# A two-layer graph network on one NeuronCore: stage 1 written out as one order on three engines, and the MLP's input transposed by DMA

## The chip, the core and the metric

The kernel runs on one core of a Trainium2 chip. The core has a matrix engine (TensorE, PE in the profile; its weight loads are PEld), three other compute engines (VectorE or DVE, ScalarE or ACT, GpSimd or POOL) and an engine that only issues DMAs here (SyncE or SP). Each engine takes its own instructions in order; engines wait for one another by semaphores. The metric is the time of one execution on the device, in microseconds (us). Three runs of the kernel before took 2258.7, 2261.97 and 2261.64 us; their median is 2261.64 us.

## The reference, cut to what matters

There are N = 3327 nodes with 1024 features. Two layers follow one another.

```python
# layer 0: a quantised graph convolution
h = relu(layernorm(x))
h_q = round(min(h / act_alpha, 1) * 15) / 15 * act_alpha
w_q = sign(wc) * round(abs(wc) * 7) / 7 * wgt_alpha   # wc = clip((w - mean(w)) / std(w) / wgt_alpha, -1, 1)
support = relu(h_q @ w_q)                             # 3327x1024 @ 1024x1024
x = x + adj @ quantise(support)                       # adj: 3327x3327
# layer 1: eight-head graph attention and an MLP
h = relu(layernorm(x))
Wh = einsum('nf,hfd->hnd', h, W)                      # 8 heads of 64
e = leaky_relu(e_src[:, :, None] + e_dst[:, None, :], 0.2)
att = softmax(where(adj > 0, e, NEG))
enc = elu(att @ Wh) laid side by side                 # 3327x512
x = x + mlp(enc)                                      # 512 -> 256 -> 256 -> 512 -> 1024, relu between
```

## The kernel before

Nodes are cut into T = 26 tiles of 128 rows. The program has four stages, one after another on PE:

1. **Stage 1, support (to about 135 us).** The weight w (1024 x 1024) is loaded as eight slices of 128 rows; its mean and variance are taken by DVE (L341) and, for slices 2 and 5, by ACT (L259 to L263). After that each slice, one 512-column half at a time, is rounded to small integers (wb, int8; ACT at L415 or DVE at L413) and clamped (w_int, bf16; DVE or GpSimd, L417 and L419). Node tiles come in pairs (GT = 2): `load` reads two tiles of x, `measure` takes their statistics on DVE, `normalise` turns these into a scale and a bias in a chain over GpSimd, ACT (root, L131) and DVE (reciprocals). `to_bytes` (ACT, L286) rounds a tile to bytes (xb), `quantise` clamps it on DVE (xq, L296) and transposes it (xqt): tile 0 by eight PE transposes (L304) and an ACT copy (L305), tiles 1 to 25 by a DMA transpose on SP. Then there are sixteen products for each tile on PE (`product`, L430: two halves of eight slices), an eviction by ACT (sb, L456) and a clamp by DVE into s_int.
2. **Stage 2 (to about 942 us)**: adj @ s_int (L568), the residual, layer norm, the transposition of each tile as two planes of 16-bit halves (`transposed_by_dma`: ACT copy yh at L475, DMA transpose, ACT copy ht at L479) and the heads' products (L502).
3. **Stage 3, attention (to about 1954 us)**: head by head, over columns in two subsets of seven and six tiles; masked rows are built by DVE (sel, L867) and multiplied by PE (acc, L876). Each of 32 closes ends in the activation of its rows and a DMA by GpSimd into enc_d, a DRAM buffer of 32-bit words [nodes, 512]. In the last steps the MLP's first group of four tiles is started in between (`first_layer`: transposes at L822, copies at L827, products at L832).
4. **Stage 4, MLP (to about 2252 us)**: seven groups, six of four tiles and one of two. For each, SP loads enc_d and the residual rows (`load_nodes`), PE transposes enc (L935, 16 for a full group) and ACT copies it to enct (L938), then `dense` three times (products at L910, eviction h by ACT at L917), and the last layer (o, L947) with the residual added by DVE (L957) and stored by SP.

What sets the order: `pin` (`tc.keep_in_program_order`) keeps an instruction in the order in which it is written on its engine. Before, the weight's instructions on ACT and DVE are pinned, the first tiles' steps stand between them by a table (`between`), and the products and later tiles are placed by the scheduler, which decides each engine's order when it builds the program. x0's normalisation (L131, L132, L138, L165, L166) is not pinned. The first three tiles' products are written half by half (half 0 of tiles 0, 1, 2, then half 1). The pool of xq tiles has 2 buffers, that of xqt 4, PSUM has 3 tiles for products and 1 for transposes.

Of the kernel before, what the change touches and what calls it, by code (L numbers as in the profile page):

```python
# [8 lines left out]
F32 = mybir.dt.float32  # L9
# [11 lines left out]
P = 128  # L21
# [4 lines left out]
F = 1024  # L26
# [34 lines left out]
def two_layer_kernel(  # L61
# [42 lines left out]
    enc_d = dram.tile([NP, EMB], F32, name="enc_d")  # L104

    const.tile([P, 152], F32, name="gap")
# [4 lines left out]
    def reciprocal(t, name):  # L111
        r = const.tile([P, 1], F32, name=name)
        nc.vector.reciprocal(r, t)
        return r

    def scaled(t, c, name):
        r = const.tile([P, 1], F32, name=name)
        nc.vector.tensor_scalar(r, t, c, None, ALU.mult)
        return r

    def load_rows(dst, ap, t):

        if rows_of(t) < P:
            nc.vector.memset(dst, 0.0)
        for r in row_pieces(t):
            nc.sync.dma_start(dst[r], ap[t * P + r.start : t * P + r.stop, :])

    def half_inverse(v, n, tag, engine=nc.vector):

        s, r, q = (small.tile([P, n], F32, tag=tag + c, name=tag + c) for c in "srq")  # L130
        nc.scalar.activation(s, v, AF.Sqrt)  # L131
        nc.vector.reciprocal(r, s)  # L132
        if n == 1:
            nc.vector.scalar_tensor_tensor(q, v, r, s, ALU.mult, ALU.add)
        else:
            engine.tensor_tensor(q, v, r, ALU.mult)
            engine.tensor_tensor(q, q, s, ALU.add)
        nc.vector.reciprocal(r, q)  # L138
        return r

    def statistics(stats, src):
        for c in range(FC):
            nc.vector.bn_stats(stats[:, c, :], src[:, c * 512 : (c + 1) * 512])

    def plus_eps(var, n, tag, engine=nc.vector):
        v = small.tile([P, n], F32, tag=tag + "v", name=tag + "v")
        engine.tensor_scalar(v, var, EPS, None, ALU.add)
        return v

    def normalised(dst, src):  # L150

        stats = small.tile([P, FC, 6], F32, tag="stats", name="stats")
        statistics(stats, src)
# [3 lines left out]
        r = half_inverse(plus_eps(mv[:, 1:2], 1, "ln"), 1, "ln")  # L157
        nc.vector.tensor_scalar(r, r, 2.0, None, ALU.mult)
        return ins, r

    def scale_and_bias(rs, mean, n, factor, tag, engine=nc.vector):

        nb = small.tile([P, n], F32, tag=f"{tag}n", name=f"{tag}n")
        if engine is nc.vector:
            nc.vector.tensor_scalar(rs, rs, factor, None, ALU.mult)  # L165
            nc.vector.scalar_tensor_tensor(nb, mean, -1.0, rs, ALU.mult, ALU.mult)  # L166
        else:
            engine.tensor_scalar(rs, rs, factor, -1.0, ALU.mult, ALU.mult)
            engine.tensor_tensor(nb, mean, rs, ALU.mult)
            engine.tensor_scalar(rs, rs, -1.0, None, ALU.mult)  # L170
        return rs, nb
# [11 lines left out]
    with tc.tile_pool(name="at", bufs=2, reuse_waits="tile") as atp:  # L183
# [35 lines left out]
        with tc.tile_pool(name="s1", bufs=2, reuse_waits="tile") as s1, tc.tile_pool(  # L219
            name="s1_mm", bufs=3, space=PSUM, reuse_waits="tile"  # L220
        ) as mm_ps, tc.tile_pool(name="s1_tp", bufs=1, space=PSUM, reuse_waits="tile") as tp_ps:
# [16 lines left out]
            def pair(t0):  # L238
                xs = s1.tile([P, GT, F], F32, name="xs", bufs=3)
                return xs, {t0 + q: xs[:, q] for q in range(GT)}  # L240

            def measure(mv, src, ordered=False, amid=lambda: None):

                stats = s1.tile([P, FC, 6], F32, name="stats1")
                for c in range(FC):
                    ins = nc.vector.bn_stats(stats[:, c, :], src[:, c * 512 : (c + 1) * 512])
                    if ordered:
                        pin(ins)
                    if c == 0:
                        amid()  # L250
                ins = nc.vector.bn_aggr(mv, stats.rearrange("p c s -> p (c s)"))
                if ordered:
                    pin(ins)

            def measure_on_scalar(mean, squares, src, name):

                junk = s1.tile([P, F], BF16, tag="xq", name="junk")
# [4 lines left out]
                junk = s1.tile([P, F], BF16, tag="xq", name="junk")  # L262
                pin(nc.scalar.activation(junk, src, AF.Square, bias=nmean, accum_out=squares))  # L263

            def normalise(xs, mv, t0, n, engine=nc.vector):

                v = plus_eps(mv[:, :n, 1], n, f"l0{n}", engine)
                r = half_inverse(v, n, f"l0{n}", engine)
                rs, nb = scale_and_bias(r, mv[:, :n, 0], n, to_q, f"l0{n}", engine)
                for q in range(n):  # L270
                    ready[t0 + q] = xs[t0 + q], rs[:, q : q + 1], nb[:, q : q + 1]

            def load(t0, ordered=False):
                _, xs = pair(t0)
                for t in xs:
                    load_rows(xs[t], x, t)
                mv = s1.tile([P, GT, 2], F32, name="mv")
                for q in range(GT):
                    measure(mv[:, q], xs[t0 + q], ordered)
                normalise(xs, mv, t0, GT, nc.gpsimd)  # L280


            def to_bytes(t, ordered=False):
                xs, rs, nb = ready.pop(t)
                xb = s1.tile([P, F], U8, name="xb")
                ins = nc.scalar.activation(xb, xs, AF.Relu, bias=nb, scale=rs)  # L286
                if ordered:
                    pin(ins)
                return xb

            def quantise(t, xb=None, ordered=False):
                if xb is None:
                    xb = to_bytes(t, ordered)

                xq = s1.tile([P, F], BF16, name="xq")
                ins = nc.vector.tensor_scalar(xq, xb, QA, None, ALU.min)  # L296
                if ordered:
                    pin(ins)

                xqt = s1.tile([P, KF, P], BF16, name="xqt", bufs=4)  # L300
                if t == 0:
                    tp = tp_ps.tile([P, KF, P], BF16, name="tp")
                    for k in range(KF):
                        nc.tensor.transpose(tp[:, k, :], xq[:, k * P : (k + 1) * P], ident_b)  # L304
                    pin(nc.scalar.copy(xqt, tp))  # L305
                else:
                    nc.sync.dma_start_transpose(xqt, xq)
                return xqt


            xs01, xs23, xs45 = (pair(t)[1] for t in (0, 2, 4))
            load_rows(xs01[0], x, 0)
            for k in range(KF):
                nc.sync.dma_start(w[:, k, :], w0[k * P : (k + 1) * P, :])
            for t, xs in ((1, xs01), (2, xs23), (3, xs23), (4, xs45), (5, xs45)):
                load_rows(xs[t], x, t)

            mv0, mv1, mv23, mv45 = (
                s1.tile([P, n, 2], F32, name=f"mv_{i}", bufs=1) for i, n in enumerate((1, 1, 2, 2))
            )  # L320
            measure(mv0[:, 0], xs01[0], ordered=True)
# [8 lines left out]
            normalise(xs01, mv0, 0, 1)  # L330
# [13 lines left out]
            xqts = {0: quantise(0, ordered=True)}  # L344
# [23 lines left out]
            nc.tensor.matmul(ps[:, 0:1], ones, w_mv[:, 0:1], start=True, stop=True)  # L368
# [16 lines left out]

            xbs = {}

            def rounded(t):  # L390
                xbs[t] = to_bytes(t, ordered=True)
# [611 lines left out]
```

## Time and profile before

The profiled execution took 2258.69 us; its span from the first to the last instruction is 2256.9 us, at a mean granted PE clock of 0.997.

| stage | from, us | to, us | main lines |
|---|---|---|---|
| start, until the first product | 0 | 29.1 | L341, L259, L415 |
| 1, support | 29.1 | 135.2 | L430 |
| 2, adj @ support and heads | 135.2 | 942 | L568, L502 |
| 3, attention | 942 | 1954 | L674, L867, L876 |
| 4, MLP | 1954 | 2252 | L910, L935, L947 |

| engine | busy us (share of the span) |
|---|---|
| PE | 2199.3 (97%) |
| DVE | 1532.4 (68%) |
| ACT | 1062.0 (47%) |
| POOL | 145.0 (6%) |

A row of the groups reads: line, engine, operation, output from inputs, shape, count, then busy time and the mean ns of one, then the engine's idle time just before these instructions with what ended most of it. A row of a timeline reads: start, time until the last of the run ends, engine, line, operation, count, and in brackets the engine's wait before it and what ended it. Starts of successive matmuls overlap with the ends of earlier ones, so the pace is taken from start to start.

### The profile page before, as it was taken

How to read it: one execution, taken by the hardware profiler on the slowest of the kernel's cores; microseconds unless marked ns; L12 is line 12 of the kernel's file. 1: busy time of each engine (PE TensorE's matmuls, PEld its weight loads, DVE VectorE, ACT ScalarE, POOL GpSimd, SP SyncE). 2: the span in 40 equal slices, each digit the busy share in tenths (PEclk: the TensorE clock that was granted, in tenths of full speed). 3: DMA queues.
4: the chain of work that ended last, by engine and by line, in shares of the span. 5: the costliest groups of instructions: out<-in, count | busy, mean ns of one | idle time of the engine just before them, and what ended most of it. 6: DMA issues, size and time to landing. Idle time of an engine off the chain costs nothing. (4 is left out here: it accounts for less than half of the span.)

```text
span 2256.9 us, 31286 instructions
## 1 busy us (share of the span) xinstructions
PE 2199.3 (97%) x12496; PEld 1753.9 (78%) x12496; DVE 1532.4 (68%) x1989; ACT 1062.0 (47%) x1642; POOL 145.0 (6%) x241
## 2 busy tenths in 40 slices
PE   4999999999999999899999999999999999999998
PEld 1466777777777677699999999999999999644444
DVE  7744555555555545588999999999999999722211
ACT  4634445544454454356555556555555555311120
POOL 1300111110111101000000000000000000000000
PEclk9999999999999999999999999999999999999999
DMA  6854656555665556934242331644242422443311
GB/s 208 206 188 132 188 176 182 159 163 170 181 182 168 157 162 188 311 125 146 85 135 89 108 120 46 221 162 147 81 147 85 140 84 76 143 139 117 121 56 56
DMA packets 228578, 324.56 MB, mean 144 GB/s; under 512 B 88452, under 2 KB 169300, under 8 KB 228432
## 3 DMA queue, kind: packets, MB, share of 16 engines
q1 hardware_dynamic: 208648, 249.39, 36.2%
q0 software_dynamic: 19776, 73.17, 9.9%
q8 instruction: 98, 1.61, 0.3%
q14 instruction: 48, 0.39, 0.1%
q10 hardware_dynamic: 8, 0.00, 0.0%
HBM read 216.07 MB, written 86.79 MB: 134 GB/s over the span
## 5 line engine op out<-in xcount | busy, mean ns | idle before, releaser
L867 DVE SCALAR_TENSOR_TENSOR sel<-srow,ndst,mask 128x896 fp32r<-128x896 f32 (+1 forms) x832 | 864.2, 1079 | 52.7 <-PE acc L876 47.2
L674 PE MATMUL mps<-dw,mf 128*128 128x260 f32 x2704 | 452.2, 283 | 0.1
L568 PE MATMUL mm<-s_int,hi 128*128 128x512 f32 x1352 | 427.1, 397 | 0.0
L568 PE MATMUL mm<-s_int,lo 128*128 128x512 f32 x1352 | 419.2, 391 | 0.0
L876 PE MATMUL acc<-f_even,sel 128*128 128x260 f32 x2704 | 400.2, 286 | 6.7 <-issue 5.0
L876 PE MATMUL acc<-f_odd,sel 128*128 128x260 f32 x2704 | 394.6, 286 | 0.0
L673 ACT CAST mf<-mask 128x1664 fp32r<-128x1664 uint8 x208 | 331.4, 1593 | 118.7 <-PE mps L674 100.7
L674 PEld LDWEIGHTS mps<-dw,mf 128*128 128x128 f32 x2704 | 377.0, 188 | 0.3 <-ACT part L678 0.3
L876 PEld LDWEIGHTS acc<-f_even,sel 128*128 128x128 f32 x2704 | 357.3, 190 | 11.7 <-issue 5.9
L876 PEld LDWEIGHTS acc<-f_odd,sel 128*128 128x128 f32 x2704 | 352.7, 188 | 7.3 <-issue 3.1
L568 PEld LDWEIGHTS mm<-s_int,hi 128*128 128x128 f32 x1352 | 253.9, 188 | 63.7 <-issue 12.0
L568 PEld LDWEIGHTS mm<-s_int,lo 128*128 128x128 f32 x1352 | 251.9, 188 | 51.3
L199 DVE TENSOR_SCALAR mk<-at 128x896 uint8<-128x896 f32 (+1 forms) x104 | 61.8, 596 | 225.3 <-DMA at<-in_adj_t 224.0
L502 PE MATMUL whm<-whead,ht 128*128 128x512 f32 x416 | 184.4, 596 | 6.9 <-ACT ht L479 6.8
L947 PE MATMUL o<-weights,h 128*128 128x512 f32 x416 | 179.7, 592 | 0.0
L947 PEld LDWEIGHTS o<-weights,h 128*128 128x128 f32 x416 | 79.0, 190 | 99.1 <-issue 99.0
L502 PEld LDWEIGHTS whm<-whead,ht 128*128 128x128 f32 x416 | 77.6, 190 | 100.9 <-issue 87.1
L194 ACT CAST hi<-at 128x896 fp32r<-128x896 f32 x104 | 92.5, 890 | 124.1 <-PE mm L568 87.6
L678 ACT COPY part<-mps 128x260 f32<-128x260 f32 x104 | 39.4, 378 | 223.1 <-PE mps L674 223.1
L198 DVE TENSOR_TENSOR lo<-at,hi 128x896 fp32r<-128x896 f32 x104 | 106.1, 1020 | 39.5 <-ACT hi L194 39.3
L957 DVE TENSOR_TENSOR yo<-o,nodes 128x1024 f32<-128x1024 f32 (+1 forms) x27 | 31.8, 1182 | 137.6 <-PE o L947 137.4
L430 PE MATMUL mm<-w_int,xqt 128*128 128x512 bf16 x416 | 96.5, 389 | 13.4 <-ACT sb L456 4.8
(157 smaller groups left out, 1559.2 us busy)
## 6 DMA issues: line engine op xcount, KB each, us to landing
feat_d<-fw POOLq DMA_DIRECT2D x26, 1040.0 KB, 5.3
f_even<-feat_d SPq DMA_DIRECT2D x7, 3380.0 KB, 12.3
f_odd<-feat_d SPq DMA_DIRECT2D x7, 3380.0 KB, 12.9
at<-in_adj_t SPq DMA_DIRECT2D x52, 448.0 KB, 3.5
at<-in_adj_t SPq DMA_DIRECT2D x52, 384.0 KB, 3.3
mask<-mask_d SPq DMA_DIRECT2D x39, 416.0 KB, 7.7
dw<-dsum_d SPq DMA_DIRECT2D x16, 910.0 KB, 8.8
dsum_d<-dw POOLq DMA_DIRECT2D x26, 520.0 KB, 6.2
```

The lines of the kernel that those rows point to most:

```text
L194: ins = nc.scalar.copy(hi, at)
L198: nc.vector.tensor_tensor(lo, at, hi.bitcast(F32), ALU.subtract)
L199: ins = nc.vector.tensor_scalar(mk[:, r], at, 0.0, None, ALU.is_gt)
L430: nc.tensor.matmul(mm[:, r], xqts[t][:, k, :], w_int[:, k, r], start=(k == 0), stop=(k == KF - 1))
L502: ins = nc.tensor.matmul(whm, ht[:, k, :], whead[:, k, :], start=(k == 0), stop=(k == KF - 1))
L568: nc.tensor.matmul(mm[:, c * 512 : (c + 1) * 512], which[:, q, :], s_int[j][:, c * 512 : (c + 1) * 512], start=(j == 0 and which is hi), s ...
L673: nc.scalar.copy(mf, mask[:, j : j + TH, :])
L674: nc.tensor.matmul(ps, mf[:, j % TH, :], dw[:, j, :], start=(j == 0), stop=(j == T - 1))
L678: nc.scalar.copy(part[:, i % 7], ps.rearrange("p (q c) -> p q c", q=2))
L867: nc.vector.scalar_tensor_tensor(sel[:, :nb], srow[:, :nb], ndst[:, j, h : h + 1], mask[:, :, j, :], ALU.is_gt, ALU.mult,)
L876: nc.tensor.matmul(accs[b], sel[:, b, :], f[:, j, :], start=(j == 0), stop=(j == T - 1))
L947: nc.tensor.matmul(ps[:, c * 512 : (c + 1) * 512], h3[:, k, q * P : (q + 1) * P], w4[:, k, c * 512 : (c + 1) * 512], start=(k == 0), stop= ...
```

## The change

**Stage 1.** Everything on PE, ACT and DVE is pinned, and the text is one sequence. x0's chain is pinned and stands before the weight statistics. The weight halves are written step by step (`round_weight`, `clamp_weight`): ACT rounds slices 0, 1, 3, 4, 6 and 7 of each half (before: 0, 1, 3, 4, 6), DVE slices 2 and 5 (before: 2, 5, 7); GpSimd clamps 1, 3, 5, 6, 7 of half 0 and 1, 3, 5, 6 of half 1, DVE the others. Between them stand the first tiles' steps. The scale of each pair is now a generator (`normaliser`) whose three parts are placed one by one, always with its small steps on GpSimd. Tile 0, tile 3 and all even tiles are transposed by PE and copied by ACT, 14 tiles in all; the other 12 by DMA (25 before). The first products are written as products(0,0), (1,0), (0,1), transposes of tile 2, (1,1), (2,0), transposes of tile 3, (2,1), with (tile, half); from t = 3 on a loop has one tile's products per turn, with the transposes of a later tile between its two halves. xq gets 3 buffers, the pairs' statistics 3, PSUM's transposes 2. The clearing of the last, incomplete tile moves from DVE to GpSimd.

```diff
-            def quantise(t, xb=None, ordered=False):
...
+            def by_tensor(t):
+                return t % 2 == 0 or t == 3
+
+            def quantise(t):
+
+                xq = xqs[t] = s1.tile([P, F], BF16, name="xq", bufs=3)
+                pin(nc.vector.tensor_scalar(xq, xbs.pop(t), QA, None, ALU.min))
+
+                xqts[t] = s1.tile([P, KF, P], BF16, name="xqt", bufs=4)
+                if not by_tensor(t):
+                    nc.sync.dma_start_transpose(xqts[t], xqs.pop(t))
+
+            def transpose(t):
+                tps[t] = tp_ps.tile([P, KF, P], BF16, name="tp")
+                xq = xqs.pop(t)
+                for k in range(KF):
+                    pin(nc.tensor.transpose(tps[t][:, k, :], xq[:, k * P : (k + 1) * P], ident_b))
+
+            def transposed(t):
+                pin(nc.scalar.copy(xqts[t], tps.pop(t)))
...
+            products(0, 1)
+            transpose(2)
+            products(1, 1)
+            measure(4)
+            to_bytes(3)
+            transposed(2)
+            quantise(3)
+            products(2, 0)
+            transpose(3)
+            products(2, 1)
+            load_pair(8)
+            measure(5)
+            support_bytes(0)
+            norm45 = normaliser(2)
+            transposed(3)
+            next(norm45)
+            support(0)
+            next(norm45)
+            measure(6)
+            next(norm45)
+            to_bytes(4)
+            support_bytes(1)
+            quantise(4)
+            support(1)
+            measure(7)
+            to_bytes(5)
+            load_pair(10)
+            norm67 = normaliser(3)
+            next(norm67)
+            quantise(5)
+            next(norm67)
+            measure(8)
+            next(norm67)
+            for t in range(3, T):
...
+                norm = None
+                if t % GT == 0 and t + 4 < T:
+                    norm = normaliser((t + 4) // GT)
+                    next(norm)
+                    next(norm)
+                if t + 6 < T:
+                    measure(t + 6)
+                if norm:
+                    next(norm)
+                support_bytes(t - 1)
+                support(t - 1)
+                if t + 3 < T:
+                    to_bytes(t + 3)
+                    if t % GT == 0 and t + 8 < T:
+                        load_pair(t + 8)
+                    quantise(t + 3)
+                products(t, 0)
+                ahead = 4 if t == 3 else t + 2
+                if ahead < T and by_tensor(ahead):
+                    transpose(ahead)
+                    transposed(ahead)
+                products(t, 1)
```

The first part of `normaliser` takes the sum with epsilon (GpSimd) and the root (ACT), the second the first reciprocal (DVE) and two GpSimd steps, the third the second reciprocal (DVE) and three GpSimd steps.

**Stages 3 and 4.** enc_d holds two planes of 16-bit halves. Each close makes one more ACT copy (eh) and two GpSimd DMAs instead of one. A group of the MLP is loaded transposed, by two DMA transposes on SP instead of four loads. ACT copies the planes together into enct, one group ahead; PE has no transposes there, neither in the groups nor in `first_layer`. In the program as built, the next group's four copies stand on ACT as two ahead of the second layer's first eviction, one between its two evictions and one behind them (for the last group of two tiles: three and one); the copies of groups 1 and 2, eight in all, stand ahead of group 1's first eviction.

```diff
-    enc_d = dram.tile([NP, EMB], F32, name="enc_d")
+    enc_d = dram.tile([2, NP, EMB], U16, name="enc_d")
...
+            eh = s3.tile([P, 7, HD], F32, tag="ex", name="eh").rearrange("p b d -> p (b d)")
+            eh = eh.bitcast(U16).rearrange("p (q n) -> p q n", q=2)[:, :, : nb * HD]
+            nc.scalar.copy(eh, halves_of_words(ht[:, :nb].rearrange("p b d -> p (b d)")))
+            for q in range(2):
+                nc.gpsimd.dma_start(
...
-                    for q, t in enumerate(range(t0, min(t0 + 4, T))):
-                        nc.sync.dma_start(enc[:, q, :], enc_d[t * P : (t + 1) * P, :])
+                    rows = slice(t0 * P, min(t0 + 4, T) * P)
+                    for q in range(2):
+                        nc.sync.dma_start_transpose(by_feature(enc, rows.stop - rows.start)[:, q], enc_d[q, rows])
...
+                following = s4.tile([P, EMB // P, 512], F32, name="enct")
+                n = (min(t0 + 8, T) - t0 - 4) * P
+                for k in range(EMB // P):
+                    nc.scalar.copy(
+                        halves_of_words(following[:, k, :n]),
+                        by_feature(enc_x1[(g + 1) % 2][0], n)[:, :, k],
+                    )
...
-                enct = s4.tile([P, EMB // P, 512], F32, name="enct")
-                for k in range(EMB // P):
-                    tp = ps_p.tile([P, 512], F32, tag="ps", name="tp4")
-                    for q, t in enumerate(tiles):
-                        nc.tensor.transpose(
-                            tp[:, q * P : (q + 1) * P], enc[:, q, k * P : (k + 1) * P], ident
-                        )
-                    nc.scalar.copy(enct[:, k, :cols], tp[:, :cols])
```

## The prediction

> **What bounds the kernel now.** I read the busy shares first, then the chain that ended last, then TensorE's own timeline. TensorE (PE) is busy for 97% of the span. The chain followed back from the last instruction reaches only through the MLP, and its rows there are PE's.
>
> ```profile
> PE 13%; ACT 0%; DVE 0%; DVEq 0%; issue 0%
> PE o L947 8%; PE h_ps L910 5%; PE tp L935 0%; ACT h L917 0%; ACT su L718 0%; DVE yo L957 0%; DVEq L1000 0%
> L430 PE MATMUL mm<-w_int,xqt 128*128 128x512 bf16 x416 | 96.5, 389 | 13.4 <-ACT sb L456 4.8
> ```
>
> So a microsecond is won only where PE waits or where it does work that can go. The groups name the first: 13.4 us of idle before L430, in stage 1. The change leaves the order of stages 2 and 3 alone. PE's timeline by start, length, count and wait shows stage 1:
>
> ```profile
> 29.13 0.59 PE L430 MATMUL mm<-w_int,xqt 128*128 128x512 bf16 x1 [3.54 <-DVE w_int L419]
> ...
> 33.81 6.54 PE L430 MATMUL mm<-w_int,xqt 128*128 128x512 bf16 x15 [0.57 <-POOL w_int L417]
> ...
> 58.44 24.42 PE L430 MATMUL mm<-w_int,xqt 128*128 128x512 bf16 x112 [1.21 <-DMA xqt<-xq]
> 83.02 3.61 PE L430 MATMUL mm<-w_int,xqt 128*128 128x512 bf16 x16 [0.16 <-ACT sb L456]
> 88.64 20.95 PE L430 MATMUL mm<-w_int,xqt 128*128 128x512 bf16 x96 [2.01 <-ACT sb L456]
> 110.69 24.82 PE L430 MATMUL mm<-w_int,xqt 128*128 128x512 bf16 x112 [1.09 <-ACT sb L456]
> 135.16 0.81 PE L568 MATMUL mm<-s_int,hi 128*128 128x512 f32 x2
> ```
>
> The reader is to see two paces. Fifteen products in 6.54 us are about 0.43 us each; 112 in 24.42 us are 0.216 each (a product's own 0.38 us end taken off). From 58.44 on stage 1 is PE at the second pace with 3.3 us of gaps (0.16 + 2.01 + 1.09). At 58.44, 80 products are done and 336 are left; 0.216 x 336 is 72.6, with the gaps 75.9, which ends at 134.3 against 135.16 seen. The sum closes to 0.9 us.
>
> The second removable thing is in the MLP:
>
> ```profile
> 2040.39 1.91 PE L935 MATMUL tp<-ident,nodes 128*128 128x128 f32 x16
> 2042.14 7.03 PE L910 MATMUL h_ps<-enct,weights 128*128 128x512 f32 x16
> 2049.01 10.84 PE L910 MATMUL h_ps<-h,weights 128*128 128x512 f32 x24
> ```
>
> Sixteen transposes hold PE for 1.75 us, start to start.
>
> **Stage 1, the start: -3.1 us at the scale, nothing by itself.** Before, x0's normalisation is behind weight statistics on DVE that wait for a DMA (3.41 us, to 10.59), so ACT's xb starts at 13.79. After, the chain is ahead of them: xb near 8.4, its transposed copy done near 14.7 instead of 17.9, ACT's weight statistics, which follow it in order, done near 19.9 instead of 23.0, and the weight scale at 24.0 instead of 27.1. The clamps of the two halves, redistributed over DVE and GpSimd, then end near 31.1 and 39.0, where the same walk of the old queues gives 37.4 and 47.8. This is cover: it is worth only what the node tiles can follow.
>
> **Stage 1, the ramp: this takes the gain back.** I walked the new written orders of ACT, DVE and GpSimd with the durations of before's rows (xb 1.24, sb 1.10, transposed copy 1.01, statistics half 0.67, clamp 0.69, root 0.20). At 39.1 PE has 24 products done. It does 16 more and the transposes of tiles 2 and 3 (16 x 0.216 + 16 x 0.056 = 4.4), to 43.7. Then, in order: ACT copies tile 3's transposition, to 44.9, and only behind that takes the root for tiles 4 and 5; DVE's second reciprocal comes behind tile 6's statistics, 46.6; three GpSimd steps; xb4 at 47.9, then sb1 to 50.2. DVE measures tile 7, to 52.2, before tiles 6 and 7 can have their root at 52.8; xb6 waits for their scale until 55.8; tile 4's copy stands **behind xb6** on ACT and ends at 58.0. Behind it on PE stand products(4,0) and everything later. In those 14.3 us PE has 24 products and 8 transposes, 5.6 us of work: it waits 2.8 us before tile 4's transposes and 6.0 us before products(4,0). At 58.0 only 64 products are done, so before is ahead by 16 products (3.5 us) at nearly the same moment.
>
> That such a chain is this slow is a row of before:
>
> ```profile
> 51.03 0.56 POOL L147 TENSOR_SCALAR l02v<-mv 128x2 f32<-128x2 f32 x1 [3.23 <-DVE mv L251]
> 51.62 0.20 ACT L131 ACTIVATE l02s<-l02v 128x2 f32<-128x2 f32 x1 [0.52 <-POOL l02v L147]
> 54.14 2.37 ACT L286 ACTIVATE xb<-xs,l02n,l02r 128x1024 uint8<-128x1024 f32 x2 [1.31 <-POOL l02r L170]
> ```
>
> From GpSimd's first step to xb are 3.1 us.
>
> **Stage 1, the rest.** 22 tiles are left: 22 x 16 x 0.216 = 76.0. Ten of them (6, 8, ... 24) are transposed on PE: 10 x 8 = 80 transposes. The row for eight takes 1.04 us at the slow pace (0.104 each between starts), so 0.056 at the fast one if it halves as a product does: 4.5 us. Per pair of tiles PE has 7.4 us, ACT about 5.6 and DVE about 5.4, so no gaps. 58.0 + 76.0 + 4.5 = 138.5 against 135.2: **+3.4 us**. The 13 DMA transposes fewer (25 to 12; 3.1 us each to landing) save PE nothing more: where PE waited for them, the gaps are already counted.
>
> Two rules weigh here. The Trainium skill, "TensorE: Matmul & The Clock Gate", section "Back-to-back issue gap", gives a sustained 81 ns for a pair of weight load and 128-column matmul: 80 x 0.081 is 6.5 instead of 4.5, and stage 1 would be +5.4. The row is at the slow pace, but the products' own rows halve (0.43 to 0.216); I take 0.056, with 0.104 (+3.8 more) as the upper end and 0.050 below. The same page, section "The HAM clock gate", says that the array falls to half pace after an idle window of about 3.4 us and needs about as much busy time to return. That speaks against this change: the 6.0 us wait would cost 3.4 us of work done at half pace, +1.7, or +3.4 if it falls twice. The trace has no wait over 2.01 us inside the run of products, and none of these slowed them. I take nothing, since the wait rests on my walk, and keep +3.4 for the range. Below, the ramp may be shorter (GpSimd steps of 0.2 instead of 0.3): stage 1 at 0 or, with no ramp wait at all, -5.
>
> **Attention.** Each close gets an ACT copy into two 16-bit planes and two GpSimd DMAs where there was one. The copy's nearest row is L475's, 1.90 us for 2048 columns; 32 copies of at most 896 columns are about 0.9 us each. ACT's casts in that stage wait 100.7 us for PE, which hides them; GpSimd is 6% busy. Uncovered, one copy late costs PE 0.9. The last tile's clearing moved to GpSimd, the third xq buffer and the second PSUM tile for transposes cost nothing: they only loosen waits.
>
> At the end of attention DVE finishes its last masked row at 1951.37 and PE's last products end near 1954.2, because the first layer of MLP group 0 and its transposes are mixed in (2.29 us of PE per row against DVE's 0.94). With 16 transposes gone, that layer finishes earlier, and the last eight rows have no MLP in between: PE ends about 1 us behind DVE, 1952.3: **-1.9** (0 to -1.9).
>
> **MLP.** 88 transposes on PE go: 5 x 1.75 and 0.9 for the last group of two tiles: **-9.65**. Certain.
>
> In their place ACT makes four copies per group out of DMA-transposed planes. Nearest row, the same kind of copy:
>
> ```profile
> L479 ACT COPY ht<-yht 128x2048 uint16<-128x2048 uint16 x25 | 62.6, 2506 | 85.5 <-DMA yht<-yh 85.5
> ```
>
> 1024 columns of it are about 1.28 us. They were hidden behind L938's (0.56 each) before; now they are one group ahead, but ACT issues in order, and the order puts two copies **before** the first eviction of the second layer, one between its two and one after. Before, the third layer starts its second step 4.57 us after the second layer begins (an eviction is 0.69 and waits 1 us for PE each time). After, the first layer's eviction (to +0.9), three copies and two evictions bring it to 5.89: 1.32 us of PE waiting in each of three groups, and 0.28 where the copies are of two tiles: **+4.24** (0 if they run early in ACT's long idle, +6 if a copy costs 1.45).
>
> Group 1's data is transposed from a buffer whose last write lands some 16 us after attention ends; two DMA transposes issued at 3.6 us each and landing in 5.8 are in at +25.4, eight copies done by +36, and its first layer starts at +39.4. Margin 3.4 us, cost nothing; each us past it is a us. Later groups have 47 us for two transposes. SP has them among the output stores that wait for DVE, in a queue with no other reader due within the group.
>
> **Sum.** +3.4 - 1.9 - 9.65 + 4.24 = -3.9. The profiled execution took 2258.69 us (span 2256.9); -3.9 gives 2254.8 there. Against the median of the runs, 2261.64, the same difference gives **2257.7**.
>
> **The rivals.**
> A, the forecast: the ramp and the ACT order both return part, -1.5 to -8.
> B, **the stall is not there**. The earlier scale and fewer SP transposes let node tiles follow: stage 1 at -1 instead of +3.4, or the copies cost nothing: -8.1 for either, and about -12.6 for both; near 2251. For it: before's ramp carries the same chain with PE idle 1.2 us only; against: tile 4's copy really stands behind xb6.
> C, **slower**: the clock falls in the 6.0 us wait. +3.4 in stage 1 at half pace and copies at 1.45 (+1.7): 2257.7 + 5.1 is 2262.8; with transposes at 81 ns (+2.0) and no gain in the last rows (+1.9) it is 2266.7. It decides once clock and copies add more than 3.9. For it: the rule; against: no row here.
> D, **the MLP's planes come late**: each of six groups waits for its transposes, so the change moves its 1.6 us per group from PE to a wait. 2257.7 + 5 is 2263. For it: one queue carries them with stores; against: 47 us per group.
>
> **How the numbers follow.** A 0.46 (0.26 beyond the bound, 0.20 within), B 0.33 (faster), C 0.12 (0.07 within, 0.05 slower), D 0.09 (0.08 within, 0.01 slower). A measurement of this kernel tells 0.2%, 4.5 us, from no change: below 2257.1 is faster. Faster 0.59, same 0.35, slower 0.06. The range holds A, most of B and C's first figure: 2247 to 2263.5.
>
> **What would show it.** PE's timeline: first product near 26 to 29, a wait of several us before products near 50 and near 58, and L568 starting at 138.5. In the groups no L935 and L822; PE's wait before the third layer of 1.3 us, released by ACT h. Products at 0.43 us after the long wait mean C. Waits for enct released by DMA mean D. An L568 start before 135 means B, and that my walk of ACT's order is wrong.

## The result and the profile after

The changed kernel takes **2252.14 us** in the median of six runs (2251.08 to 2254.14), the kernel before 2261.69 (2258.7 to 2261.97). The ratio is 0.9961, with a 95% interval of 0.9948 to 0.9974: 9.5 us less by the medians, 8.8 by the ratio. The profiled execution took 2251.08 us, its span is 2249.2; against the profiled execution of before (2258.69) that is -7.6. Each of the two is the lowest of its kernel's six runs, so the rest of the 9.5 lies between these runs and the medians.

The chain that ended last, from the page, and then the group of stage 1's products, from the groups by line:

```profile
PE 53%; ACT 1%; DVE 0%; DMA 0%; issue 0%; DVEq 0%
PE acc L977 27%; PE mps L770 13%; PE o L1048 8%; PE h_ps L1011 4%; ACT enct L1033 0%; PE h_ps L933 0%; DMA weights<-in_w1t 0%; ACT h L1018 0%; DVE sel L968 0%; DVE nodes L1044 0%; ACT su L814 0%; DVE su L811 0%; DVE yo L1058 0%; ACT rest L941 0%; DVEq L1101 0%
```

```profile
L308 PE MATMUL mm<-w_int,xqt 128*128 128x512 bf16 x406 | 97.6, 395 | 14.0 <-ACT xqt L300 5.7 <-DVE w_int L430 4.4 <-DMA xqt<-xq 2.9
```

PE still carries the chain, L935's and L822's transposes are gone, and the idle before stage 1's products is 14.0 us where it was 13.4: the waits were moved, not removed. PE's timeline shows where to:

```profile
47.83 0.62 PE L297 MATMUL tp<-ident_b,xq 128*128 128x128 bf16 x8 [2.36 <-DVE xq L287]
48.29 1.89 PE L308 MATMUL mm<-w_int,xqt 128*128 128x512 bf16 x7
55.92 3.60 PE L308 MATMUL mm<-w_int,xqt 128*128 128x512 bf16 x8 [5.74 <-ACT xqt L300]
59.31 1.03 PE L297 MATMUL tp<-ident_b,xq 128*128 128x128 bf16 x8
60.16 6.87 PE L308 MATMUL mm<-w_int,xqt 128*128 128x512 bf16 x31
67.08 0.61 PE L297 MATMUL tp<-ident_b,xq 128*128 128x128 bf16 x8
...
138.25 0.81 PE L664 MATMUL mm<-s_int,hi 128*128 128x512 f32 x2
```

The reader is to see three things. The two waits of the ramp are there, 2.36 us and 5.74 us. Behind the second one eight products take 3.60 us and eight transposes 1.03, about twice what such rows take elsewhere (eight transposes 0.61 to their end lower down, 0.45 from start to start). And from 60 us on there is no wait at all; stage 2 begins at 138.25, 3.1 us later than before.

Where the 7.6 us come from is found by taking the same event in both traces. The differences (after less before) are: +3.1 at stage 2's first product; +2.6 at attention's first product (945.14 against 942.53); +1.6 thirty us into attention (974.35 against 972.75), +1.7 near its end; +1.15 at the first product behind attention; -7.8 at the last group's last layer (2229.65 against 2237.46). So the MLP gives 9.0, the end of attention 0.5, stage 1 takes 3.1, and 1.5 appears in stage 2 and the turn to attention, where the change alters nothing on PE.

Of this 1.5 us, 1.0 lies in the first thirty us of attention, and there the granted clock differs. A row of the next view reads: the stretch, its length, PE's busy time with its instructions, the granted PE clock, the busy share of the DMA engines and what they moved in GB/s. The first row is of the kernel before, the second of the changed one:

```profile
940.48:950.72 10.24, 7.72 (x33) 0.50 1.05 388
944.22:951.05 6.83, 5.44 (x22) 0.50 1.06 387
```

The clock is at half for 10.24 us in the one trace and for 6.83 in the other. A second trace of the changed kernel (e5 below) has 10.24 too: it is 2.4 us behind the kernel before at stage 2's first product, 2.85 at attention's and 2.7 thirty us later, while the MLP gives 9.0 and the end of attention 0.6 again. So the 1.5 us belong to one execution and not to the change.

At the end of attention's step before the last, PE waits for ACT's evictions, which it did not before:

```profile
1927.71 3.21 PE L977 MATMUL acc<-f_odd,sel 128*128 128x260 f32 x24 [1.05 <-ACT xs L992]
```

In the MLP, PE's timeline and then ACT's in group 1:

```profile
2001.67 11.09 PE L1011 MATMUL h_ps<-h,weights 128*128 128x512 f32 x24
2012.59 27.63 PE L1048 MATMUL o<-weights,h 128*128 128x512 f32 x64
...
2137.45 10.85 PE L1011 MATMUL h_ps<-h,weights 128*128 128x512 f32 x24
2148.14 27.63 PE L1048 MATMUL o<-weights,h 128*128 128x512 f32 x64
```

```profile
2002.45 2.51 ACT L1033 COPY enct<-nodes 128x1024 uint16<-128x1024 uint16 x2
2004.84 0.67 ACT L1018 ACTIVATE h<-h_ps,rest 128x512 f32<-128x512 f32 x1
2005.41 1.33 ACT L1033 COPY enct<-nodes 128x1024 uint16<-128x1024 uint16 x1
2006.60 0.68 ACT L1018 ACTIVATE h<-h_ps,rest 128x512 f32<-128x512 f32 x1
2007.17 1.33 ACT L1033 COPY enct<-nodes 128x1024 uint16<-128x1024 uint16 x1
```

The copies stand where I had them and take 1.25 us each, but a group with them costs PE 10.92 us from the second layer's start to the last layer's, a group without them 10.69: 0.24 us, not 1.32.

### The profile page after: what moved, and what is told of

The parts are those of the page before. It is cut to its first block, busy times and chain, and to the rows that moved or that the text cites. A ratio compares the mean times of both kernels' runs of the same rounds, so it can differ in the third digit from the quotient of the medians.

```text
span 2249.2 us, 31329 instructions
## 1 busy us (share of the span) xinstructions
PE 2192.3 (97%) x12486; PEld 1749.2 (78%) x12496; DVE 1532.7 (68%) x1976; ACT 1118.3 (50%) x1689; POOL 182.0 (8%) x286
## 4 chain that ended last, share of the span: by engine, by line
PE 53%; ACT 1%; DVE 0%; DMA 0%; issue 0%; DVEq 0%
PE acc L977 27%; PE mps L770 13%; PE o L1048 8%; PE h_ps L1011 4%; ACT enct L1033 0%; PE h_ps L933 0%; DMA weights<-in_w1t 0%; ACT h L1018 0%; DVE sel L968 0%; DVE nodes L1044 0%; ACT su L814 0%; DVE su L811 0%; DVE yo L1058 0%; ACT rest L941 0%; DVEq L1101 0%
## 5 line engine op out<-in xcount | busy, mean ns | idle before, releaser
L839 POOL DMA_DIRECT2D enc_d<-eh x64 | 57.5, 903 | 935.9 <-ACT eh L837 876.3
L1018 ACT ACTIVATE h<-h_ps,rest 128x512 f32<-128x512 f32 (+1 forms) x54 | 35.1, 653 | 195.8 <-PE h_ps L1011 195.8
## 6 DMA issues: line engine op xcount, KB each, us to landing
f_even<-feat_d SPq DMA_DIRECT2D x7, 3380.0 KB, 13.4
```

The lines of the kernel that those rows point to most:

```text
L839: nc.gpsimd.dma_start(enc_d[q, sub[0] * P : (sub[-1] + 1) * P, h * HD : (h + 1) * HD].rearrange("(b p) d -> p b d", p=P), eh[:, q].rearran ...
```

## The experiments

The runs, with the ratio to the kernel before that ran beside them, and two events of each trace (us):

| run | median | ratio, 95% interval | stage 2 begins | attention begins |
|---|---|---|---|---|
| before (first profile) | 2261.69 | | 135.16 | 942.53 |
| changed | 2252.14 | 0.9961, 0.9948 to 0.9974 | 138.25 | 945.14 |
| e1 MLP alone | 2250.95 | 0.9955, 0.9943 to 0.9968 | 134.22 | 945.03 |
| e2 stage 1 alone | 2262.09 | 1.0008, 1.0000 to 1.0016 | 138.61 | 946.07 |
| e3 copy of tile 4 early | 2249.86 | 0.9953, 0.9941 to 0.9966 | 136.04 | 945.99 |
| e4 PE kept busy | 2254.03 | 0.9973, 0.9963 to 0.9984 | 135.76 | 946.32 |
| e5 changed, again | 2252.08 | 0.9964, 0.9952 to 0.9977 | 137.55 | 945.38 |
| e6 layers in order | 2255.52 | 0.9982, 0.9974 to 0.9991 | 137.18 | 945.06 |
| e7 copies behind, held | 2259.16 | 0.9997, 0.9989 to 1.0005 | 137.80 | 945.79 |
| e8 tiles by DMA | 2254.21 | 0.9973, 0.9961 to 0.9984 | 130.29 | 948.31 |
| e9 both moved | 2247.48 | 0.9941, 0.9929 to 0.9954 | 132.43 | 942.02 |
| e10 e8, started late | 2253.98 | 0.9969, 0.9958 to 0.9980 | 138.26 | 946.75 |
| e11 old stage 1, MLP moved | 2250.25 | 0.9952, 0.9938 to 0.9965 | 135.93 | 946.53 |

**The two halves alone.** e1 is the kernel before with the hunks of the closes and the MLP; e2 is the changed kernel with those hunks taken back (its first hunk is shown).

```diff
-    enc_d = dram.tile([2, NP, EMB], U16, name="enc_d")
+    enc_d = dram.tile([NP, EMB], F32, name="enc_d")
...
```

> The kernel before with the change of attention's closes and of the MLP alone; stage 1 stays as it was. If the two parts add up (my reading of the two traces): the gain of the changed kernel's part behind stage 1 is kept (about -7.5 in the last attention step and the MLP, and -1.5 or nothing in the stages between), and stage 1's +3.1 us is absent, so about 2250 us in the median, 0.994 to 0.996 of before, and the first product of stage 2 at 135. The rival, that the rewritten stage 1 is what gains (the end of stage 2 and the start of attention were 1.5 us nearer in the changed kernel's trace), gives 2255 or more.

> The changed kernel with the old closes and the old MLP, so the new stage 1 alone. If the parts add up: stage 2's first product at 138.2 instead of 135.2, nothing won behind it, so about +3 us, 2263 to 2265, ratio 1.001. The rival, that stage 1's new order makes up its loss in stage 2 and at the turn to attention (the difference between the traces shrank there from +3.1 to +1.6), gives 2261 to 2263, not to be told from before.

e1 came to 0.9955, -10.2 us by the ratio (-9.3 by the medians); e2 to 1.0008, +1.8 us with an interval from 0 to +3.6. By the ratios their sum is -8.4, where the changed kernel has -8.8. So all of the gain is the MLP's and the closes', and the rewritten stage 1 costs something or nothing. e2 lies between its two readings: stage 2 began at 138.61 as expected, yet attention at 946.07.

**Is ACT's order the wait, and is the slow pace the clock?** e3 moves tile 4's copy ahead of tile 6's rounding:

```diff
             to_bytes(5)
+            products(3, 0)
+            transpose(4)
+            transposed(4)
             load_pair(10)
...
-                products(t, 0)
-                ahead = 4 if t == 3 else t + 2
-                if ahead < T and by_tensor(ahead):
+                if t > 3:
+                    products(t, 0)
+                ahead = t + 2
+                if t > 3 and ahead < T and by_tensor(ahead):
```

> The changed kernel with one step moved: tile 3's first products, tile 4's transposes and ACT's copy of them stand in the written order ahead of the root for tiles 6 and 7 and of tile 6's rounding, behind tile 5's rounding. If ACT's order is what made PE wait 5.74 us (my step), products of tile 4 start near 50.5 instead of 55.9; PE then waits before tile 6's transposes until that tile is clamped near 55.7, the second half of tile 4 starts near 56.2 instead of 60.2, and stage 2 starts at 134.3 instead of 138.25: -4.0 us on the changed kernel. The rival, that the node tiles' supply (statistics, root, reciprocals) sets the pace and the copy is only where it shows, moves the wait without shortening it: stage 2 starts at 137 to 138.5.

e4 leaves the order and fills the wait with products that nothing reads:

```diff
                 products(t, 1)
+                if t == 3:
+                    mms[4] = mm_ps.tile([P, F], F32, tag="mm", name="mm")
+                    for i in range(26):
+                        pin(
+                            nc.tensor.matmul(
+                                mms[4][:, :512], xqts[3][:, i % KF, :], w_int[:, i % KF, :512], start=True, stop=True
+                            )
+                        )
```

> The changed kernel with 26 further products of tile 3 by half 0 on PE, behind that tile's own and ahead of tile 4's, into a PSUM tile that tile 4's products start anew; they fill the 5.74 us wait with 5.6 us of work that nothing reads. If the eight products of tile 4 that took 3.60 us (0.43 each) and the transposes that took 1.03 us ran at half pace because PE had stood still, they now run at 0.216 and 0.056: 1.7 + 0.5 = 2.2 us less, and stage 2 starts near 136.1 instead of 138.25. If that pace had another cause (data or a wait that the records miss), stage 2 starts at 138.2 or, where the added work ends behind tile 4's copy, later.

PE's timeline of e4, then of e3:

```profile
49.59 5.78 PE L556 MATMUL mm<-w_int,xqt 128*128 128x512 bf16 x26
55.49 1.90 PE L308 MATMUL mm<-w_int,xqt 128*128 128x512 bf16 x8
57.23 0.61 PE L297 MATMUL tp<-ident_b,xq 128*128 128x128 bf16 x8
```

```profile
47.90 0.62 PE L297 MATMUL tp<-ident_b,xq 128*128 128x128 bf16 x8 [2.36 <-DVE xq L287]
48.36 3.75 PE L308 MATMUL mm<-w_int,xqt 128*128 128x512 bf16 x16
55.82 0.62 PE L297 MATMUL tp<-ident_b,xq 128*128 128x128 bf16 x8 [3.71 <-DVE xq L287]
56.28 8.76 PE L308 MATMUL mm<-w_int,xqt 128*128 128x512 bf16 x32
64.87 0.61 PE L297 MATMUL tp<-ident_b,xq 128*128 128x128 bf16 x8
```

In e4 the same eight products take 1.90 us instead of 3.60 and the transposes 0.61 instead of 1.03; stage 2 begins at 135.76, 2.5 us sooner. PE was slow because it had stood still; 2.2 were expected. (Programs that share a written stage 1 began stage 2 at 137.18 to 138.61, so that event alone is good to about 0.7; the two rows are the proof.) The whole did not gain from it: e4 took 2254.03 us, 0.9973, and reached attention at 946.32; in stage 2 PE waited 9.3 us for ht (the transposed tile that the heads' products read) where the changed kernel waits 7.1. In e3 the wait before products(4,0) is gone: tile 4's first half runs inside the 3.75 us. But the 3.71 us wait at tile 6 brings the slow pace again: 32 products take 8.76 us where 7.07 is usual, 1.7 more. I had left that out, so stage 2 begins at 136.04 and not at 134.3. ACT's order was the wait's cause; the supply behind it is the next one.

It is not the length of a wait that decides. The granted clock shows it, in two neighbouring stretches each of the changed kernel, e1, e8 and e10:

```profile
49.93:53.35 3.42, 0.25 (x2) 1.00 0.82 261
53.35:56.76 3.41, 0.84 (x3) 0.50 0.81 125
46.67:50.09 3.42, 1.37 (x6) 1.00 0.00 0
50.09:53.50 3.41, 3.39 (x9) 0.50 1.01 246
52.68:56.09 3.41, 1.10 (x6) 1.00 1.00 172
56.09:59.50 3.41, 3.03 (x8) 0.50 0.75 157
54.67:58.08 3.41, 1.42 (x7) 1.00 0.46 95
58.08:61.50 3.42, 3.42 (x18) 1.00 1.00 258
```

The wait that reaches into the first stretch is 5.74 us in the changed kernel, 1.49 in e1 (behind shorter ones), 2.69 in e8 and 2.23 in e10, and only e10 keeps its clock. In each of the thirteen traces the granted clock changes only at whole multiples of 3.413 us from its first change. Of the stretches between these multiples that were at full clock (up to 2235 us), half clock followed all 24 in which PE was busy for less than 1.4 us, 3 of the 9 between 1.4 and 1.6, and none of the 7972 above. So what counts in these traces is PE's work within one such stretch. Where the stretches fall differs from execution to execution: the changed kernel's second trace (e5) lost its clock from 48.74 us on, behind the 2.38 us wait at tile 4's transposes, where the first one kept it until 53.35.

**Why the copies cost so little.** e6 holds the three dense layers' products in the written order.

```diff
-                    nc.tensor.matmul(
+                    tc.keep_in_program_order(
+                        nc.tensor.matmul(
...
```

> The changed kernel with PE's products of the MLP's first three layers held in the order in which they are written (block by block, both steps of a block together); ACT's order stays. In the changed kernel PE lost only 0.24 us to the copies in each of three groups, where I had 1.32. My reading of the weight loads: PE's built order puts the first step of the third layer's second block ahead of the first block's second step, 0.86 us of work that covers the wait. If so, holding the order brings the wait back: 0.24 + 0.86, about 1.1 us per group, the three groups 46.1 instead of 45.26 from last-layer start to last-layer start, +2.6 in all. The rival, that the evictions behind the copies come early enough anyway and my 1.32 was simply too large, leaves the groups at 45.26.

> The changed kernel unaltered, as the standard for the runs beside it. By both theories 0.995 to 0.997 of before; stage 2's first product at 138.2 to 138.6, since stage 1 is written out as one order and came to 138.25 and 138.61 in two programs that share it.

e5 repeats the changed kernel's time (2252.08), but its stage 2 began at 137.55, sooner than the 138.2 to 138.6 that I expected. PE's timeline of e6 in group 1:

```profile
2002.10 5.04 PE L1012 MATMUL h_ps<-h,weights 128*128 128x512 f32 x10
2007.78 6.28 PE L1012 MATMUL h_ps<-h,weights 128*128 128x512 f32 x14 [0.64 <-ACT h L1020]
2013.89 27.63 PE L1050 MATMUL o<-weights,h 128*128 128x512 f32 x64
```

A wait for ACT's eviction appears in each of the three groups, which take 46.12 us instead of 45.26: 0.86 more, exactly one step of one block (two passes of 0.43). The whole is 3.4 us slower than the changed kernel beside it (2255.52 against 2252.08); 2.6 are these groups, and 0.4 is the last group, which holds no copies and takes 36.89 instead of 36.50. So the scheduler had put another block's step into the wait.

**The copies moved.** e7 pins all evictions of the MLP and writes the copies behind the third layer's; it also pins the evictions before the last step of attention ahead of the first group's copies.

```diff
+                    tc.keep_in_program_order(
+                        nc.scalar.copy(
+                            halves_of_words(following[:, k, :n]),
...
+                if i == len(attends) - 2:
+                    tc.keep_in_program_order(ins)
```

> The changed kernel with two steps of ACT moved: the next group's four copies stand behind the third layer's evictions, in the last layer's time, instead of around the second layer's; and the four copies for the first group stand behind the evictions of the step before the last of attention, instead of ahead of them. If the copies cost 0.24 us in each of three groups, these go from 45.26 to 45.02 (-0.75 in all). If the copies ahead of the evictions are what made PE wait 1.05 us there and shifted the end of attention by 1.3, that comes back: PE's first product behind attention 1.3 us nearer to its place before. Together -2.0 us. The rival for the second: the wait for the first layer's weights (1.23 us, a DMA) or DVE's rows set the end, and it stays where it was: -0.75.

PE's timeline of e7 at the first group:

```profile
1957.69 3.70 PE L1015 MATMUL h_ps<-rest,weights 128*128 128x512 f32 x8 [0.61 <-ACT xs L994]
1967.34 8.95 PE L1015 MATMUL h_ps<-h,weights 128*128 128x512 f32 x16 [5.95 <-ACT h L1023]
```

It was 7 us slower than the changed kernel, for a reason in neither theory: being pinned, group 0's evictions stand on ACT behind the last close, PE waits 5.95 us for them, and the 16 products behind it take 8.95 us instead of 7.13, the slow pace again. The part asked for is readable all the same: later groups take 45.01 instead of 45.26, and the evictions at the end of attention's step before the last come 31.4 us after the preceding ones as they did in the kernel before, instead of 32.7. But the last step did not end sooner for it (61.5 us from the same event to the first product behind attention, in the changed kernel 61.5 too): the first layer's products, started later, stand in PE's way at its end. The rival was right there.

**Fewer transposes on PE.** e8 is e3 with this line:

```diff
-                return t % 2 == 0 or t == 3
+                return t in (0, 2, 3, 4)
```

> The changed kernel with tile 4's copy moved forward as before (which ended at 136.04), and tiles 6, 8, ... 24 transposed by DMA instead of PE: only tiles 0, 2, 3 and 4 by PE. It takes 80 transposes from PE (-4.5 us, 0.445 for eight) and the 3.71 us wait ahead of tile 6's transposes together with the half pace behind it (-1.7), and adds waits for DMA transposes, which took 5.4 us to land here, with tiles rounded three ahead of their products. If the transposes on PE were the price of sure supply and DMA keeps up: stage 2 starts at 129 to 131. The rival, that DMA transposes come late (before had 3.3 us of such gaps with tiles four ahead): waits at most tiles, stage 2 at 133 or later.

PE's timeline of e8, and a row of its groups by line:

```profile
56.47 74.17 PE L308 MATMUL mm<-w_int,xqt 128*128 128x512 bf16 x336 [2.69 <-DMA xqt<-xq]
130.29 0.81 PE L668 MATMUL mm<-s_int,hi 128*128 128x512 f32 x2
```

```profile
L602 PE MATMUL whm<-whead,ht 128*128 128x512 f32 x416 | 187.4, 604 | 14.2 <-ACT ht L579 14.1
```

Stage 1 is what was expected and better than the rival had it: behind one wait of 2.69 us, 336 products without another, stage 2 at 130.29, 8 us sooner than in the changed kernel. (The slow pace was expected to go and did not: the first seven of these products took 0.43 us each, as the clock's row above shows.) Yet the kernel is 2.1 us slower than the changed one beside it. Stage 2 takes 818.0 us instead of 806.9. The last row says where most of it goes: PE waits 14.1 us at the heads' products for ht, where the changed kernel waits 7.1. Those tiles come through a DMA transpose, and in nine of them (issued from 195 to 322 us and from 788 to 884 us) the time from its issue to ACT's copy was 6.6 to 7.9 us, and 9.8 in the last, where the others have some 5.5. Most of the rest is the clock: behind the last of these waits it is at half, and sixteen of the heads' products take 9.98 us instead of 7.1. PE's timeline and the clock's row show it:

```profile
927.56 9.98 PE L602 MATMUL whm<-whead,ht 128*128 128x512 f32 x16 [3.15 <-ACT ht L579]
926.49:933.31 6.82, 5.75 (x7) 0.50 1.02 369
```

The same two terms explain stage 2's length in all thirteen traces. Less PE's wait for ht it is 799.8 to 801.4 us in the ten whose clock stays whole until PE's last wait before attention, 802.2 in the two with one stretch of 3.41 us at half (e1, e3) and 803.9 in e8 with two.

e10 is e8 with 37 products that nothing reads at the end of stage 1.

```diff
+            idle = mm_ps.tile([P, F], F32, tag="mm", name="mm")
+            for i in range(37):
+                pin(
+                    nc.tensor.matmul(
...
```

> The kernel with tiles by DMA, whose stage 2 began at 130.29 and reached attention's first product at 948.31 (818.0 us; the changed kernel took 806.9), with 37 further products that nothing reads behind stage 1's last one, 8.0 us of PE work, so that stage 2 begins at 138.3 again. If stage 2's end hangs on a chain that does not start earlier with PE (DMA transposes and loads, which PE waits for at its heads), the 8 us cost nothing there: attention at 946 to 949, stage 2 in 808 to 811. The rival: this program's stage 2 is longer by itself (its DMA transposes take 6.6 to 7 us in many tiles, wherever PE starts), so the 8 us are added: attention near 956.

Stage 2 began at 138.26 and attention at 946.75: 8 us of added work on the engine that is 97% busy cost nothing (2253.98 against 2254.21). PE's wait for ht was 7.9 us, and the clock stayed whole. Stage 2 of e8 is 9.5 us longer than e10's: 6.2 at the wait for ht, most of the rest at the clock. So e8 gave its 8 us back there. That an earlier start makes the transposes slow is not shown: e9 below starts stage 2 almost as early, waits 8.5 us for ht and keeps 3.1 of the 5.8 us that it is ahead of the changed kernel. Every trace has one or two runs of two to five tiles with slow transposes (issued at 168 and 200 us in the kernel before, from 388 to 485 in e10), beside the last tile, which is slow in all. The changed kernel, e2, e3, e5, e6 and e7 have them at the same place, from about 570 to 670 us, so the place is not chance. What makes them slow was not found.

**A version that is faster.** e9 takes e3, puts a later tile's transposes behind both halves of the products, so that tile 4's second half does not wait for tile 6, and moves the MLP's copies from group 1 on only. e11 has the old stage 1 and the same move in the MLP.

```diff
-                ahead = t + 2
-                if t > 3 and ahead < T and by_tensor(ahead):
-                    transpose(ahead)
-                    transposed(ahead)
                 products(t, 1)
+                ahead = t + 2
+                if t > 3 and ahead < T and by_tensor(ahead):
+                    transpose(ahead)
+                    transposed(ahead)
...
+                    if g:
+                        tc.keep_in_program_order(ins)
```

> The changed kernel with tile 4's copy moved forward, the transposes of a later tile behind both halves of a tile's products instead of between them, and the next group's copies behind the third layer's evictions from group 1 on. In stage 1 tile 4's second half no longer stands behind tile 6's transposes: the wait there shrinks from 3.71 to about 2 us (then tile 5's DMA transpose and tile 6's clamp are due) and the half pace behind it is absent, so stage 2 starts near 132.5 instead of 136.04 (-1.7 and -1.7). MLP groups 45.02 instead of 45.26, -0.75. If these add up on the whole: -6.5 against the changed kernel, 0.9935 of before. The rival, from the runs so far (stage 2 reached attention at 945 to 948 whether it began at 130 or at 138): what stage 1 gains is lost ahead of attention, and only the MLP's 0.75 and 1 to 2 us more are left, 0.9950 to 0.9960 of before.

> The kernel before with the new closes and the new MLP, the next group's copies behind the third layer's evictions from group 1 on: the run of the MLP alone (0.9955 of before, groups 45.26 where copies stood between) with that one move. Groups at 45.02: -0.75, about 0.9952 of before. The rival, that moved copies come too late for the next group's first layer, shows as a PE wait for enct there and no gain.

PE's timeline of e9:

```profile
55.50 0.62 PE L297 MATMUL tp<-ident_b,xq 128*128 128x128 bf16 x8 [0.44 <-DVE xq L287]
56.06 7.08 PE L308 MATMUL mm<-w_int,xqt 128*128 128x512 bf16 x31
62.98 0.61 PE L297 MATMUL tp<-ident_b,xq 128*128 128x128 bf16 x8
...
132.43 0.81 PE L668 MATMUL mm<-s_int,hi 128*128 128x512 f32 x2
```

e9 is the fastest kernel of the study: 2247.48 us, 0.9941; its five runs end at 2249.32, below the lowest of the changed kernel's in either set (2251.08), though these ran at other times. Stage 2 begins at 132.43 (132.5 expected), and the groups take 45.01. In the parts of stage 1 it came otherwise than expected: the wait at tile 6 is 0.44 us where I had about 2, with the pace behind it whole, but the clock fell behind the 2.38 us wait at tile 4, from 48.94 to 52.36 us, which cost about 1.5 in seven products at 0.43. Against the changed kernel it is -4.6 of the -6.5 that adding up would give: stage 2 took 809.6 us here, 2.7 more than in the changed kernel. e11's groups take 45.01 too; 0.9952 beside e1's 0.9955 is the expected sign and too little to tell.

## Why the prediction was right, and where its sum was not

The time, 2252.14, lies in the range (2247 to 2263.5) and moved the way that was forecast, but by 9.5 us where I had 3.9. Step by step, from the two profiled executions (-3.9 forecast, -7.6 found):

- **Stage 1, +3.4; found +3.1.** The mechanism is as told: the copy of tile 4 stood behind tile 6's rounding, and PE waited 2.36 and 5.74 us (2.8 and 6.0 forecast). Two errors cancelled, so that the number came out is luck. My walk was 2 us late: products(4,0) began at 55.92, not at 58.0, because the weight's scale was ready sooner (ACT's first rounding of a half began at 21.61, where I had the scale at 24.0) and all that follows moved with it. And I took nothing for the clock, which cost 2.1 in the two rows (1.70 in the products, 0.42 in the transposes; e4). The Trainium skill's rule ("TensorE: Matmul & The Clock Gate", "The HAM clock gate") of half pace after an idle window held against the row that I preferred; I should have counted it, since my own walk had a wait longer than any row of the trace before. The runs go further than that rule: the clock fell behind waits of 1.49 us (e1) and 2.69 us (e8) too, with up to 1.4 us of work in the stretch of 3.41.
- **The transposes on PE, 0.056 each: right.** Eight of them take 0.445 us from start to start. The 81 ns of the skill's "Back-to-back issue gap" is not seen here.
- **The end of attention, -1.9; found -0.5.** The step before the last lost 1.3 us: the four copies of the first group, which I had not counted, stand on ACT ahead of the evictions, and PE waits 1.05 us for these. The last step itself gained 1.8.
- **The MLP's transposes, -9.65; found about -9.7** (9.0 of gain and 0.75 of waits). Right.
- **The copies, +4.24; found +0.75.** This is the term that was mis-sized. "1.32 us of PE waiting in each of three groups" took PE's order to be that of the kernel before. The eviction is late by nearly what I had (4.9 us from the second layer's start to that eviction's start, where before had 3.8), but the built order has 0.86 us of another block's work there, and 0.24 is left (e6 brings back 0.86). The small group's 0.28 was not seen at all. This alone is 3.5 of the 3.7 us between forecast and trace; the end of attention (1.4 less won than forecast) and the next item (1.5 more) cancel, again by luck.
- **Stages 2 and 3, nothing; found -1.5** up to the last steps, and not found again in the same kernel's second trace (e5: +0.3). The 1.0 at the turn to attention is one stretch of 3.41 us less at half clock. In all thirteen traces the first thirty us of attention take 30.0 to 30.4 with three such stretches at half (six traces) and 28.3 to 29.7 with two (seven). "Nothing" stands.

Rival B was put on "stage 1 at -1 or the copies free"; its second half is what happened, its first is not. Rival C's mechanism, the clock, was there, and was paid for by a walk that was too late. D was not: the chain touches enct and one DMA with 0% each, and group 1's data was copied by 1987.7 for a first layer at 1994.80, a margin of 7 us where I had 3.4.

## What to carry to other kernels

A wait on the matrix engine can cost more than its length: in these traces the clock fell to half behind every stretch of 3.41 us with less than 1.4 us of work, whether the idle time was one wait of 5.74 us or one of 1.49 behind shorter ones. So add up the idle time around a wait, fill it with work, and look for the one instruction in an in-order queue that stands behind somebody else's late input, as tile 4's copy did. Before pricing a copy that is put ahead of an eviction, check the consumer's order too: a scheduler may have other work for the gap. And a gain in one stage is worth only what the next stage can pass on; 8 us won in stage 1 (e8) came out as nothing and 5.8 (e9) as 3.1, which the event at the next stage's end shows and the stage's own timeline does not.

## What was not expected of the hardware

The length of a wait does not tell whether PE's clock falls. It was at half behind waits of 1.49 us (e1), 2.00 (e11, where eight products from 90.20 us on took 0.43 each), 2.38 (e9) and 2.69 (e8), and stayed whole behind waits of 2.36 (changed kernel), 2.37 and 2.23 us (e10). It falls and rises on a grid of 3.41 us, and the changed kernel lost 2.1 us to 6.83 at half, e3 1.7 to 3.41, and e7 1.8 to 6.83, part of which PE stood still. DMA transposes of 512 KB that mostly reach their reader in 5.5 us take about 7 in runs of a few neighbouring tiles. With the clock this sets how long stage 2 takes, and so how much of an earlier start survives.
